# Two graph-attention layers on one core: the last block's norm moved behind the first turns of x1, sums of quarters moved off the masks, the last pair in another order

## The chip, the cores and the metric

The kernel runs on one core of a Trainium2 chip. The metric is the device time of one execution in microseconds (us), as the median of several runs. The profile shows one such execution: its span is measured from the first to the last recorded event, and the execution's own time is a little longer.

## The reference, cut to what matters

x is 4096 x 512 and adj is a 4096 x 4096 matrix of zeros and ones. Layer 0 takes, for each row, the mean over its first 64 neighbours, applies one linear map to that mean and another to the row itself, and normalises the sum. Layer 1 is an attention over all neighbours, with a residual and a norm.

```python
# layer 0
keep = Ab & (cumsum(Ab, axis=1) <= 64)
cnt = keep.sum(axis=1)
xj = leaky_relu((keep @ X) / max(cnt, 1) @ W_nb.T + b_nb)
xi = leaky_relu(X @ W_line.T + b_line)
x1 = layernorm(x + xi + where(cnt > 0, xj, 0))
# layer 1
Wh = x1 @ W + bW
e = leaky_relu((Wh @ a1 + b1)[:, None] + (Wh @ a2 + b2)[None, :], 0.2)
out = layernorm(x1 + softmax(where(adj > 0, e, -9e15), axis=1) @ Wh)
```

## The kernel before

The 4096 rows are 32 blocks of 128; two blocks make a pair (block b holds the even or the odd rows of pair b // 2). The order of work is written out by hand: each engine runs its instructions in the order of the program, and a DMA queue issues in order too. Tiles come from pools with a fixed number of buffers; a new tile waits until the last user of its buffer, or of the memory that it overlaps, is done. The stages are these.

**Layer 0.** First, y = x W_nb.T is computed block by block (L340) and kept in SBUF as a high and a low part, y_hi and y_lo. Meanwhile the adjacency is read, its running count is scanned on DVE (L179), and the kept edges are packed to bytes in DRAM (code_d). Then, for each of 32 blocks, PE multiplies the 0/1 matrix with y_hi and y_lo (L502, 64 products in four groups of 8 x 2). While block i is on PE, `finish(i - 1, g)` is run for g = 0 to 3 on DVE: mean, bias and bend (L462, L465), the sum with the block's own row, which SP loaded from own_d (L469, L497), statistics (`ln_stats`, L115, whose power -0.5 runs on POOL, L123), the scaling (L128) and the store to x1_d by POOL (L476), and two dot products with the folded attention vectors (L481), which go to the tile e12. The last block's finish is written after the loop (L509 to L510), when PE has no more products of layer 0.

**Layer 1, the slices.** The pools of layer 1 use the memory of layer 0 again. `front` holds the weights `ws` and four slots `x1s` of slices of x1. SP loads the weights (L534), the bias row bias_w (L538), and the slices (`load_turned`, four DMAs each, L553). DVE first adds the counts and writes e12's last parts (L755 to L762); POOL writes e2 and the row statistics to DRAM and reads them back as e2_n and st_n (L763 to L771), because the masks need e2 along the free dimension. Then, for 32 slices s (L780 to L805):

- PE multiplies slice s, turned, with the weights: four products of 512 columns (L786; the profile shows two records for each);
- `finish_wh(s - 1)` adds the bias on DVE (L575). For every second group of four slices it also forms the four sums of quarters of Wh (L580 to L583) that the Strassen-like products need;
- `turn_x1(s + 2)` turns a slice on DVE (L566) into one of two buffers;
- in slices 8 to 15, `mask` and `score` work on the first two blocks' weights: ACT expands the byte mask (L604), DVE subtracts it from e2_n and reduces to the maximum (L607), ACT bends the score (L596). In slices 12 to 19 `weigh` takes exponentials on ACT (L649), four slices behind; `greatest` and `shift` (L613 to L642) join the maxima of a block before its first weighing;
- in slices 22 and 26 `turn` (L668) and `combine` (L681 to L684) prepare the first two parts of the pair 0.

**Layer 1, the parts.** Each of 16 pairs has four parts q (L808 to L838). `consume(q)` runs seven products of four steps on PE (L707), which add up in four PSUM banks: products 1 and 2 share a bank, 4 and 7, 5 and 6, and 3 has its own. Next to it, DVE and ACT mask, score, weigh and turn later blocks. A pair's result is summed (`end_low`, `end_top`), divided by the sum of weights, added to the residual row (loaded by `load_res`), normalised and written (`end_row`).

**The end.** The last pair's sums and its two rows are written after the loop (L839 to L843). Its seven products stand in an order of their own:

```python
order = (1, 2, 4, 7, 5, 6, 3) if q < NP * NT - 1 else (1, 2, 6, 7, 5, 4, 3)
```

Of the kernel before, what the change touches and what calls it, by code (L numbers as in the profile page):

```python
# [20 lines left out]
P = 128  # L21
# [11 lines left out]
def two_layer_adj_gnn(  # L33
# [41 lines left out]

    two = const.tile([P, 1], F32, name="two")
    nc.vector.memset(two, 2.0)
    steep = const.tile([P, 2], F32, name="steep")
    nc.vector.memset(steep[:, 0:1], -0.5 * STEEP)
    nc.vector.memset(steep[:, 1:2], -1.5 * STEEP)  # L80
    far = const.tile([P, 1], F32, name="far")
    nc.vector.memset(far, FAR)
    neg_half = const.tile([P, 1], F32, name="neg_half")
    nc.vector.memset(neg_half, -0.5)

# [24 lines left out]

    code_d = [dram.tile([P, N // 2], BF16, name=f"code_d{b}") for b in range(NB)]

    def ln_stats(y):  # L115
        st = stat.tile([P, nc.vector.BN_STATS_DIM], F32, name="st")
        nc.vector.bn_stats(st, y)  # L117
        mv = stat.tile([P, nc.vector.BN_AGGR_DIM], F32, name="mv")
        nc.vector.bn_aggr(mv, st)
        ve = stat.tile([P, 1], F32, name="ve")  # L120
        nc.vector.tensor_scalar_add(ve, mv[:, 1:2], EPS)  # L121
        rs = stat.tile([P, 1], F32, name="rs")
        nc.gpsimd.tensor_tensor(rs, ve, neg_half, ALU.pow)  # L123
        return mv, rs
# [9 lines left out]
    with ExitStack() as l0:  # L134
# [5 lines left out]
        make_identity(nc, ident)  # L140

        late = big.tile([P, 3, C], F32, name="late")
        wa_row, bias_nb = late[:, 0:2, :], late[:, 2, :]

# [110 lines left out]
        with ExitStack() as la:  # L255
# [9 lines left out]
            def load_turned_x(i):  # L265

                if i < NB:
                    xrs[i] = late[:, i % 3, :].rearrange("p (j c) -> p j c", c=P)
                    for n in range(NC):
                        nc.gpsimd.dma_start(  # L270
                            xrs[i][ts(n, SQ)],
                            x_blk(i)[:, ts(n, P)].rearrange("(j a) c -> a j c", a=SQ),
                        )
# [36 lines left out]
            for k in range(2):  # L310
                t = early("left")
                raw["w"] += [t[:, c, :] for c in range(NC // 2)]
            rows = []
            for k in range(2):
                t = early("edge")
                rows += [t[:, c, :] for c in range(NC // 2)]

# [28 lines left out]
            def load_rows(queue):  # L346
                for k, src in enumerate((a1, a2, b_w)):
                    queue.dma_start(rows[k], src.partition_broadcast(P))
                queue.dma_start(b12[:, 0:1], b1.partition_broadcast(P))
                queue.dma_start(b12[:, 1:2], b2.partition_broadcast(P))  # L350

            def fold_w():
                for c in range(NC + 1):
                    wn = raw["w"][c] if c < NC else rows[2]
                    for k in range(2):
                        nc.vector.scalar_tensor_tensor(
                            rows[3], wn, 1.0, rows[k], ALU.mult, ALU.mult,
                            accum_out=wa[:, k, c : c + 1] if c < NC else ca[:, k : k + 1],
                        )
                nc.vector.tensor_tensor(ca, ca, b12, ALU.add)  # L360
                nc.sync.dma_start(wa_d.rearrange("k (c p) -> p k c", p=P), wa)

            def load_late():
                nc.gpsimd.dma_start(bias_nb, b_nb.partition_broadcast(P))
                nc.gpsimd.dma_start(
                    wa_row.rearrange("p k c -> p (k c)"),
                    wa_d.rearrange("k c -> (k c)").partition_broadcast(P),
                )

# [81 lines left out]
        def load_kt(b):  # L451
            if b < NB:
                assert done[0] > NCH * (b + 1) and not late_q
                ktbs[b] = ktb_p.tile([P, NT, P], BF16, name="ktb")
                nc.sync.dma_start_transpose(ktbs[b], code_d[b])

        def finish(i, g):
            if i < 0:
                return
            if g == 0:  # L460
                t = work.tile([P, C], F32, name="t")
                nc.vector.scalar_tensor_tensor(  # L462
                    t, accs.pop(i), rcnt[:, i : i + 1], bias_nb, ALU.mult, ALU.add
                )
                nc.vector.scalar_tensor_tensor(t, t, 0.01, t, ALU.mult, ALU.max)  # L465
                fin[i] = t
            elif g == 1:
                t, y = fin[i], owns.pop(i)
                nc.vector.scalar_tensor_tensor(  # L469
                    y, t, some[:, i : i + 1], y, ALU.mult, ALU.add  # L470
                )
                fin[i] = y, ln_stats(y)
            elif g == 2:
                y, stats = fin[i]
                ln_apply(y, stats)
                nc.gpsimd.dma_start(x1_blk(i), y)  # L476
            else:
                y, _ = fin.pop(i)
                for k in range(2):
                    junk = work.tile([P, C], F32, name="junk", bufs=1)  # L480
                    nc.vector.scalar_tensor_tensor(  # L481
                        junk, y, 1.0, wa_row[:, k, :], ALU.mult, ALU.mult,
                        accum_out=e12[:, 1 - k, i : i + 1],
                    )
# [3 lines left out]
        for s in range(NB * NS):  # L488
# [6 lines left out]
            if g == 2:  # L495
                owns[i] = work.tile([P, C], F32, name="own")
                nc.sync.dma_start(owns[i], own_d[i])  # L497
            kt = kts.pop(s)
# [9 lines left out]
            codes_step(start + int((s + 1) * RATE / NS))  # L508
        for g in range(NS):  # L509
            finish(NB - 1, g)  # L510

# [16 lines left out]
    NP = 4  # L528
    front = wp.tile([P, NI, NS * SQ], F32, name="w")
    ws = front[:, 0:2, :].rearrange("p a (b c) -> p (a b) c", c=C)  # L530
    x1s = front[:, 2:4, :].rearrange("p a (b c) -> p (a b) c", c=C)

    for n in range(NC):
        nc.sync.dma_start(  # L534
            ws[ts(n, SQ), :, :], w[ts(n, P), :].rearrange("(m b) c -> b m c", b=SQ)
        )
    bias_w = ep.tile([P, C], F32, name="res")
    nc.sync.dma_start(bias_w, b_w.partition_broadcast(P))  # L538
# [24 lines left out]
    def turn_x1(s):  # L563
        if s < NS:
            x1ts[s] = ep.tile([P, C], F32, name="c").rearrange("p (m i) -> p m i", i=P)
            nc.vector.transpose(  # L566
                x1ts[s].rearrange("p m (j a) -> p j m a", a=SQ),
                x1s[:, s % 4, :].rearrange("p (j m b) -> p j m b", m=NC, b=SQ),
            )

    def finish_wh(s):
# [6 lines left out]
        )  # L578
        if h == 1:
            nc.vector.tensor_tensor(b[:, 4], b[:, 1], b[:, 0], ALU.subtract)  # L580
            nc.vector.tensor_tensor(b[:, 5], b[:, 3], b[:, 4], ALU.subtract)
            nc.vector.tensor_tensor(b[:, 6], b[:, 5], b[:, 2], ALU.subtract)
            nc.vector.tensor_tensor(b[:, 1], b[:, 3], b[:, 1], ALU.subtract)  # L583
# [14 lines left out]
    def mask(b, i):  # L598

        if i == 0:  # L600
            wts[b] = wp.tile([P, NI, NS * SQ], F32, name="w")
            m4s[b] = stat.tile([P, NI], F32, name="m4", bufs=2)
# [90 lines left out]
    def consume(q):  # L693
# [7 lines left out]

        order = (1, 2, 4, 7, 5, 6, 3) if q < NP * NT - 1 else (1, 2, 6, 7, 5, 4, 3)
        for n in order:
# [9 lines left out]
    def load_res(g):  # L713

        for b in (2 * g, 2 * g + 1):
            x1rows[b] = ep.tile([P, C], F32, name="res")
            nc.sync.dma_start(x1rows[b], x1_blk(b))
# [9 lines left out]
    def end_low(g):  # L727

        p = banks[g]
        top = ep.tile([P, 2, HC], F32, name="c")  # L730
        low = ep.tile([P, 2, HC], F32, name="c")
        nc.scalar.copy(top[:, 0], p[1])
# [20 lines left out]


    cnt, idle = cnts[:, 0, :], cnts[:, 1, :]  # L755
    nc.vector.tensor_tensor(cnt, cnt, idle, ALU.add)
# [15 lines left out]


    for s in range(4):
        load_turned(s)
    load_nat(0, 0)
    load_nat(0, 1)
    turn_x1(0)
    turn_x1(1)
    for s in range(NS):  # L780
        if s > 0:
            load_turned(s + 3)
        pws[s] = ps_acc.tile([P, C], F32, name="acc")
# [5 lines left out]
        if s > 0:  # L789
            finish_wh(s - 1)  # L790
        turn_x1(s + 2)
        if FIRST <= s < FIRST + 8:
# [9 lines left out]
        if s in (FIRST + 14, FIRST + 18):  # L802
            q = (s - FIRST - 14) // 4
            turn(q)
            combine(q)  # L805
    finish_wh(NS - 1)

    for q in range(NP * NT):  # L808
# [17 lines left out]
        if b < NB:  # L826
            shift(b)
            for i in range(NI):
                weigh(b, i)
        if k == 0 and g > 0:  # L830
            end_weights(g - 1)
            end_low(g - 1)
            end_top(g - 1)
        if k == 1:
            if g > 0:
                end_row(2 * g - 2, nc.gpsimd)
                end_row(2 * g - 1, nc.gpsimd)
            load_res(g)  # L838
    end_weights(NT - 1)  # L839
    end_low(NT - 1)  # L840
    end_row(NB - 1, nc.scalar)
    end_top(NT - 1)
    end_row(NB - 2, nc.sync)  # L843

# [33 lines left out]
```

## Time and profile before

| what | value |
|---|---|
| median of 3 runs | 1620.12 us (1619.28 to 1620.49) |
| the profiled execution's own time | 1619.29 us |
| its span | 1617.5 us |
| PE busy | 1584.3 us (98%) |
| DVE busy | 1328.7 us (82%) |
| ACT busy | 902.5 us (56%) |
| POOL busy | 257.7 us (16%) |
| mean granted PE clock | 0.996 |

A busy share is an average over stages. Where the PE is busy without a gap, only fewer or shorter products would save time; where it has gaps, the wait that ended last tells what held it. A row of a timeline shows the start, the time from the start of the first to the end of the last instruction that was merged into it, engine, line, operation, tiles and shapes, and in brackets the engine's idle time before it with what released it. "SPq" rows are issues of DMAs by SP: their time is that of issuing, not of the transfer.

### The profile page before, as it was taken

The numbers are of one execution on the slowest core, as the hardware profiler recorded it, in microseconds if no ns is written. First come the engines' busy times: TensorE is split into PE (matmuls) and PEld (weight loads), VectorE is DVE, ScalarE is ACT, GpSimd is POOL, SyncE is SP. The second block draws the span as 40 slices with busy tenths as digits, with TensorE's granted clock in tenths as the row PEclk, the third lists the DMA queues.
The fourth block names the chain that finished last, engine by engine and source line by source line (L and its number), as shares of the span: only waits on it lengthen the run. The fifth ranks groups of instructions, "written<-read, shape, count | busy, mean of one in ns | idle before, by whom it ended". The sixth has DMA issues, their size and how long they took to land.

```text
span 1617.5 us, 18487 instructions
## 1 busy us (share of the span) xinstructions
PE 1584.3 (98%) x6456; PEld 1220.1 (75%) x6456; DVE 1328.7 (82%) x2183; ACT 902.5 (56%) x1054; POOL 257.7 (16%) x395
## 2 busy tenths in 40 slices
PE   9999999999999999989899999999999999999997
PEld 5444448888888787854358888888888888888886
DVE  4999987999999999847787778788888788788763
ACT  2655556677676766413337555567555567555520
POOL 4455532222222221120000000000000000000000
PEclk9999999999999999999999999999999999999999
DMA  8887878767776876352311111111111111111100
GB/s 194 282 260 240 260 210 241 217 196 210 220 212 194 217 205 187 92 130 79 92 46 27 53 40 53 40 27 53 53 40 53 40 28 52 53 40 53 40 7 33
DMA packets 168205, 192.74 MB, mean 119 GB/s; under 512 B 101376, under 2 KB 134176, under 8 KB 159920
## 3 DMA queue, kind: packets, MB, share of 16 engines
q1 hardware_dynamic: 147968, 131.51, 30.1%
q0 software_dynamic: 19712, 59.27, 10.7%
q8 instruction: 50, 0.82, 0.2%
q10 hardware_dynamic: 432, 0.79, 0.1%
q14 instruction: 43, 0.35, 0.1%
HBM read 132.65 MB, written 42.08 MB: 108 GB/s over the span
## 4 chain that ended last, share of the span: by engine, by line
PE 70%; DVE 20%; DMA 4%; issue 3%; ACT 2%; POOL 1%; SPq 0%; POOLq 0%; DVEq 0%; ACTq 0%
PE acc L707 34%; PE pt L707 14%; PE acc L340 9%; PE acc L502 9%; DVE left L179 8%; PE acc L786 4%; DVE left L184 2%; DVE junk L481 2%; DMA a<-in_adj_dram 1%; DVE st L117 1%; DVE own L469 1%; DMA late<-in_x_dram 1%; DVE t L465 1%; DVE t L462 1%; POOL rs L123 1%
## 5 line engine op out<-in xcount | busy, mean ns | idle before, releaser
L502 PE MATMUL acc<-y_hi,kt 128*128 128x512 f32 x1016 | 396.0, 390 | 3.1 <-ACT kt L249 3.1
L502 PE MATMUL acc<-y_lo,kt 128*128 128x512 f32 x1016 | 395.3, 389 | 0.0
L707 PE MATMUL acc<-bt,s 128*128 128x256 f32 x1536 | 342.3, 379 | 0.0
L707 PEld LDWEIGHTS acc<-bt,s 128*128 128x128 f32 x1536 | 291.8, 190 | 39.7
L604 ACT ACTIVATE w<-nat,far 128x1024 f32<-128x1024 uint8 x128 | 136.9, 1135 | 291.6 <-DVE a L668 238.9
L123 POOL TENSOR_TENSOR rs<-ve,neg_half 128x1 f32<-128x1 f32 x64 | 76.0, 1187 | 1026.5 <-DVE ve L121 1026.5
L707 PE MATMUL acc<-bt,a 128*128 128x256 f32 x1024 | 231.6, 379 | 0.0
L707 PE MATMUL pt<-bt,a 128*128 128x256 f32 x1024 | 231.5, 379 | 0.0
L502 PEld LDWEIGHTS acc<-y_hi,kt 128*128 128x128 f32 x1016 | 190.7, 188 | 44.9 <-ACT kt L249 5.3
L502 PEld LDWEIGHTS acc<-y_lo,kt 128*128 128x128 f32 x1016 | 190.7, 188 | 39.4
L707 PEld LDWEIGHTS pt<-bt,a 128*128 128x128 f32 x1024 | 194.6, 190 | 26.9 <-issue 0.5
L707 PEld LDWEIGHTS acc<-bt,a 128*128 128x128 f32 x1024 | 194.6, 190 | 26.5
L668 DVE STREAM_TRANSPOSE a<-w 128x1024 f32<-128x1024 f32 x128 | 153.0, 1225 | 59.4 <-ACT w L649 52.7
L167 ACT ACTIVATE edge<-a,steep 128x2048 bf16<-128x2048 int32 x64 | 127.9, 1998 | 104.5 <-DVE left L184 82.4
L249 ACT ACTIVATE kt<-ktb,steep 128x1024 fp32r<-128x1024 uint8 x124 | 139.4, 1147 | 82.0 <-PE acc L502 64.9
L596 ACT ACTIVATE w<-w,st_n 128x1024 f32<-128x1024 f32 x128 | 149.4, 1233 | 50.7 <-DVE m L607 50.7
L607 DVE CUSTOM_DVE_ANT_0 w<-e_n,w 128x1024 f32<-128x1024 f32 x128 | 149.5, 1221 | 4.3 <-ACT w L604 2.9
L649 ACT ACTIVATE w<-w,nm 128x1024 f32<-128x1024 f32 x128 | 145.4, 1137 | 11.3 <-DVE nm L640 11.3
L179 DVE TENSOR_TENSOR_SCAN left<-two,edge 128x2048 bf16<-128x2048 f32 x32 | 141.3, 4417 | 12.0 <-ACT edge L167 10.9
L179 DVE TENSOR_TENSOR_SCAN left<-two,ends,edge 128x2048 bf16<-128x2048 f32 x32 | 143.2, 4476 | 0.0
L786 PE MATMUL acc<-w,c 128*128 128x512 f32 x256 | 113.6, 602 | 14.9 <-DVE c L566 14.9
L202 ACT CAST code<-left 128x2048 uint8<-128x2048 bf16 x64 | 120.6, 1884 | 7.6 <-DVE left L184 7.6
(114 smaller groups left out, 1529.3 us busy)
## 6 DMA issues: line engine op xcount, KB each, us to landing
a<-in_adj_dram SPq DMA_DIRECT2D x64, 1024.0 KB, 6.0
code_d<-code POOLq DMA_DIRECT2D x64, 256.0 KB, 5.3
nat<-code_d SPq DMA_DIRECT2D x256, 64.0 KB, 2.0
own_d<-xb POOLq DMA_DIRECT2D x32, 256.0 KB, 6.0
own<-own_d SPq DMA_DIRECT2D x32, 256.0 KB, 2.7
x_d<-own POOLq DMA_DIRECT2D x32, 256.0 KB, 2.6
w<-x_d SPq DMA_DIRECT2D x128, 64.0 KB, 2.0
res<-x_d SPq DMA_DIRECT2D x32, 256.0 KB, 2.8
```

Source lines behind the costliest of these rows:

```text
L167: nc.scalar.activation(edge_of[s], loaded.pop(s), AF.Sigmoid, bias=steep[:, 0:1], scale=STEEP, accum_out=cnts[:, h, b : b + 1],)
L179: nc.vector.tensor_tensor_scan(left, two.to_broadcast([P, CH]), e, NEIGHBORS + 2.0 if h == 0 else end, ALU.max, ALU.subtract,)
L249: nc.scalar.activation(kts[s], bytes_.rearrange("p t (i r) -> p t r i", r=2), AF.Sigmoid, bias=steep[:, 1:2], scale=STEEP,)
L340: nc.tensor.matmul(pl, lhs_t[:, k, :], w_t[name][:, k, :], start=(k == 0), stop=(k == NC - 1),)
L502: nc.tensor.matmul(accs[i], kt[:, k // 2, k % 2, :], term[:, j, :], start=(j == 0 and term is y_hi), stop=(j == NB - 1 and term is y_lo),)
L596: nc.scalar.activation(dst, src, AF.Prelu, bias=bias, scale=scale, alpha=0.2)
L604: nc.scalar.activation(w_i, nats[b, i // 2].bitcast(U8)[:, i % 2, :], AF.Relu, bias=far, scale=-FAR)
L607: nc.vector.tensor_tensor_reduce(w_i, e2_n, w_i, 1.0, -3e38, ALU.subtract, ALU.max, m4s[b][:, i : i + 1])
L649: nc.scalar.activation(w_i, w_i, AF.Exp, bias=nms[b][:, i : i + 1], accum_out=z4s[g][:, r, i : i + 1])
L668: nc.vector.transpose(a[:, r].rearrange("p s (i a) -> p i s a", a=SQ), wts[2 * g + r][:, :, ts(k, 8 * SQ)].rearrange("p i (s x) -> p i s x ...
L707: nc.tensor.matmul(banks[g][n], lhs[:, j, :], bt[:, 4 * k + j, rhs, :], start=(k == 0 and j == 0 and n == mate[0]), stop=(k == NP - 1 and ...
L786: nc.tensor.matmul(pws[s], x1t[:, m, :], ws[:, m, :], start=(m == 0), stop=(m == NC - 1))
```

## The change

Five things change. First, the norm of the last block: after the loop of layer 0 nothing is finished any more. Instead, after the definitions of layer 1, SP loads the first four slices, then block 31's own row, then the first masks; DVE turns slices 0, 1 and 2; and only then `finish(31, g)` follows, with temporary rows in a tile `early` of layer 1, whose first halves take the three turned slices. Second, turned slices have three buffers (a pool `rows`, which in layer 0 holds the three rows that were the tile `late`), and a slice is turned three ahead; its load is issued seven ahead. Third, `finish_wh` only notes the quarter; the four sums are formed by `combine_wh`, once in each slice from 16 on other than 22 and 26, and what is left after block 2's weighing in part 0. Fourth, in the last part product 4 comes first, `end_weights` before the end, and the last pair's sums and norms are written out: the upper row is worked on in halves, between the steps of the lower row, and is written by two DMAs. Fifth, small moves: constants in one tile, wa_row in two loads, residual rows of even blocks in `rows`.

```diff
+    rows = ctx.enter_context(tc.tile_pool(name="rows", bufs=3, reuse_waits="tile"))
+    late = [rows.tile([P, C], F32, name="c") for _ in range(3)]
+    wa_rows, bias_nb = late[0:2], late[2]
...
             def load_late():
                 nc.gpsimd.dma_start(bias_nb, b_nb.partition_broadcast(P))
-                nc.gpsimd.dma_start(
-                    wa_row.rearrange("p k c -> p (k c)"),
-                    wa_d.rearrange("k c -> (k c)").partition_broadcast(P),
-                )
+                for k in range(2):
+                    nc.gpsimd.dma_start(wa_rows[k], wa_d[k].partition_broadcast(P))
...
             if g == 2:
-                owns[i] = work.tile([P, C], F32, name="own")
-                nc.sync.dma_start(owns[i], own_d[i])
+                if i < NB - 1:
+                    owns[i] = place("own")
+                    nc.sync.dma_start(owns[i], own_d[i])
...
-        for g in range(NS):
-            finish(NB - 1, g)
...
     front = wp.tile([P, NI, NS * SQ], F32, name="w")
+    early = wp.tile([P, NI, NS * SQ], F32, name="w")
+    spare += [early[:, i, C:] for i in (0, 2, 3)]
+    owns[NB - 1] = early[:, 1, C:]
...
     def turn_x1(s):
         if s < NS:
-            x1ts[s] = ep.tile([P, C], F32, name="c").rearrange("p (m i) -> p m i", i=P)
+            t = early[:, s, :C] if s < 3 else rows.tile([P, C], F32, name="c")
+            x1ts[s] = t.rearrange("p (m i) -> p m i", i=P)
...
         if h == 1:
+            later.append(kk)
+
+    later = []
+
+    def combine_wh():
+
+        if later:
+            b = bt[:, later.pop(0)]
             nc.vector.tensor_tensor(b[:, 4], b[:, 1], b[:, 0], ALU.subtract)
             nc.vector.tensor_tensor(b[:, 5], b[:, 3], b[:, 4], ALU.subtract)
             nc.vector.tensor_tensor(b[:, 6], b[:, 5], b[:, 2], ALU.subtract)
...
-        order = (1, 2, 4, 7, 5, 6, 3) if q < NP * NT - 1 else (1, 2, 6, 7, 5, 4, 3)
+        order = (1, 2, 4, 7, 5, 6, 3) if q < NP * NT - 1 else (4, 1, 2, 6, 7, 5, 3)
...
+    for s in range(4):
+        load_turned(s)
+    nc.sync.dma_start(owns[NB - 1], own_d[NB - 1])
+    load_nat(0, 0)
+    load_nat(0, 1)
+    for s in range(3):
+        turn_x1(s)
+        load_turned(s + 4)
+    for g in range(4):
+        finish(NB - 1, g)
...
-    turn_x1(0)
-    turn_x1(1)
     for s in range(NS):
-        if s > 0:
-            load_turned(s + 3)
...
-        turn_x1(s + 2)
+        turn_x1(s + 3)
+        load_turned(s + 7)
...
+        elif s >= FIRST + 8:
+            combine_wh()
     finish_wh(NS - 1)
...
+        while q == 0 and later:
+            combine_wh()
...
+        if q == NP * NT - 1:
+            end_weights(g)
...
-    end_weights(NT - 1)
-    end_low(NT - 1)
-    end_row(NB - 1, nc.scalar)
-    end_top(NT - 1)
-    end_row(NB - 2, nc.sync)
+    p, rz = banks[NT - 1], rzs[NT - 1]
+    top, low = (rows.tile([P, 2, HC], F32, name="c") for _ in range(2))
+    x_top, x_low = x1rows[NB - 2].rearrange("p (h c) -> p h c", h=2), x1rows[NB - 1]
+    stt = nc.vector.scalar_tensor_tensor
+    st = stat.tile([P, 2, nc.vector.BN_STATS_DIM], F32, name="st2", bufs=1)
+    nc.scalar.copy(top[:, 0], p[1])
+    tt(top[:, 1], top[:, 0], p[6], ALU.add)
+    tt(top[:, 0], top[:, 0], p[2], ALU.add)
+    tt(low[:, 0], top[:, 1], p[7], ALU.add)
+    stt(top[:, 0], top[:, 0], rz[:, 0:1], x_top[:, 0], ALU.mult, ALU.add)
+    nc.vector.bn_stats(st[:, 0], top[:, 0])
+    tt(low[:, 1], low[:, 0], p[5], ALU.add)
+    tt(low[:, 0], low[:, 0], p[4], ALU.subtract)
+    y_low = low.rearrange("p h c -> p (h c)")
+    stt(y_low, y_low, rz[:, 1:2], x_low, ALU.mult, ALU.add)
+    low_stats = ln_stats(y_low)
+    tt(top[:, 1], top[:, 1], p[5], ALU.add)
+    stt(top[:, 1], top[:, 1], rz[:, 0:1], x_top[:, 1], ALU.mult, ALU.add)
+    stt(top[:, 1], p[3], rz[:, 0:1], top[:, 1], ALU.mult, ALU.add)
+    nc.vector.bn_stats(st[:, 1], top[:, 1])
+    mv, rs = ln_rs(st)
+    ln_apply(y_low, low_stats)
+    nc.scalar.dma_start(out_blk(NB - 1), y_low)
+    for h in range(2):
+        ln_apply(top[:, h], (mv, rs))
+        (nc.sync, nc.scalar)[h].dma_start(out_blk(NB - 2)[:, ts(h, HC)], top[:, h])
```

## The prediction

> **What bounds the kernel now.** I read the page first: PE is busy for 1584.3 of 1617.5 us, so only its gaps can be saved. Its row for the products of layer 1's first stage names a gap and who ended it:
>
> ```profile
> L786 PE MATMUL acc<-w,c 128*128 128x512 f32 x256 | 113.6, 602 | 14.9 <-DVE c L566 14.9
> ```
>
> The timeline of PE from 700 to 842 us puts these 14.9 us in place. The bracket is the idle time before the row and what ended it; 8 records are one slice of x1.
>
> ```profile
> 713.38 53.33 PE L786 MATMUL acc<-w,c 128*128 128x512 f32 x120 [7.72 <-DVE c L566]
> 768.28 3.70 PE L786 MATMUL acc<-w,c 128*128 128x512 f32 x8 [1.58 <-DVE c L566]
> ...
> 786.72 20.87 PE L786 MATMUL acc<-w,c 128*128 128x512 f32 x48 [0.65 <-DVE c L566]
> 809.36 14.00 PE L786 MATMUL acc<-w,c 128*128 128x512 f32 x32 [1.77 <-DVE c L566]
> 823.55 10.57 PE L786 MATMUL acc<-w,c 128*128 128x512 f32 x24 [0.19 <-DVE c L566]
> ```
>
> The same stretch of DVE, and of SP, shows what came before the first turn:
>
> ```profile
> 705.70 0.75 DVE L462 SCALAR_TENSOR_TENSOR t<-acc,rcnt,late 128x512 f32<-128x512 f32 x1 [8.34 <-PE acc L502]
> ...
> 712.62 1.29 DVE L566 STREAM_TRANSPOSE c<-w 128x512 f32<-128x512 f32 x2
> 718.67 0.71 DVE L566 STREAM_TRANSPOSE c<-w 128x512 f32<-128x512 f32 x1 [4.76 <-PE acc L786]
> ```
>
> ```profile
> 705.46 0.35 SPq L538 DMA_DIRECT2D res<-in_L_gnn_bW_dram  x1
> 705.86 7.74 SPq L553 DMA_DIRECT2D w<-x_d  x16
> 713.64 6.12 SPq L591 DMA_DIRECT2D nat<-code_d  x8
> ```
>
> SP's rows are the catch. The load of bias_w (L538) takes space that y_hi held, so it waits for layer 0's last products (705.4), and all turned loads of x1 stand behind it. The changed program's order of instructions has that wait still, on the same product. Last, DVE at the end:
>
> ```profile
> 1604.30 0.42 DVE L733 TENSOR_TENSOR c<-c,acc 128x256 f32<-128x256 f32 x1 [17.76 <-PE acc L707]
> ...
> 1605.97 0.42 DVE L735 TENSOR_TENSOR c<-c,acc 128x256 f32<-128x256 f32 x1 [0.80 <-PE acc L707]
> ...
> 1613.70 0.55 DVE L128 TENSOR_SCALAR c<-c,mv,rs 128x512 f32<-128x512 f32 x1 [0.73 <-POOL rs L123]
> ```
>
> From 834 us to 1607.7 PE has no gap: 64 parts of 12.08 us. Nothing there is to be saved.
>
> **Part 1, the transition.** Removed from ahead of the first turn: the norm of block 31 and the counts, 705.70 to 712.6. In its place the first turn waits for its four loads. Of the 16 issues (7.74 us, 0.48 each) slice 0's last goes at 707.3 and lands some 2.9 us later: 710.2. With a turn of 0.65, PE starts at 710.9 instead of 713.38. Slice 1 lands at about 711.4, slice 2 at 713.4; the third turn ends at 714.05. Only then can DVE begin the norm (705.70 before). Block 31's own row is now issued behind the 16 (713.64) and lands 2.7 later, 716.3, where L469's successor would want it at 715.55: 0.75 lost. The norm's 6.1 us and the counts' 0.8 then end at 721.7, turn 3 at 722.4.
>
> PE: slice 0 took 5.2 us before (713.38 until the turn at 718.67, which waits for its end), the later ones 3.435. [...] The new gap is 5.2 us[...]. Cold: slices 0 to 2 end at 716.1, 719.5, 723.0, and slice 3 starts at 723.0. Warm: they end by 721.2 and slice 3 waits for turn 3 until 722.4. [...] Slice 4 needs turn 4, whose load is issued behind the eight loads of nat. Before, it landed at 725.7, which gives turn 4 at 726.7 with 0.35 of SP's added issue; if those loads land faster, since e2's small writes move from 713 to 722, PE decides, 725.9 to 726.4. I take slice 4 at 726.6. Before it was 728.97. **Gain 2.4 us, bounds 1.8 to 3.1**, not 7.7.
>
> The norm is 8.35 us later, and behind it on DVE and POOL stand e2's writes and loads. Before: L762 ended at 712.7, the first load of e2_n issued at 720.78, the last landed at about 726.6, 13.9 later. Now 721.7 + 13.9 = 735.6. The first mask reads e2_n at 746.77 - 2.4 = 744.4. It is covered by 8.8 us. The x1 store stays ahead of e2 on POOL; x1's last quarter is read only from slice 24.
>
> **Part 2, the masks (slices 8 to 31).** On the old clock, E(s) being the end of slice s: E(8) = 746.14, and 23 slices of 3.435 would end at 825.15; the next stage starts at 833.96. So 8.8 us are lost. Two things work against them. A third buffer lets turn s+3 run when slice s has ended, so a turn may be late by 6.2 us instead of 2.7. And the four sums of a quarter (L580 to L583, 1.59 us from start to start) leave slices 13 to 16, to run from 16 on.
>
> What does not go: with weighing, the mask steps are a circle DVE reduce, ACT score, ACT weigh, ACT mask, each waiting for the last: 768.85 to 773.56 is 4.71 us, with DVE idle 0.67 before each L607. Without the sums DVE merely idles longer. The reduces stay at 761.06, 768.85, 773.56, 778.27. Turns 16 to 19 then end at 766.6, 771.25, 775.95, 780.65 (L575 0.6, turn 0.65), against slices due at 770.2, 773.6, 777.0, 780.5: PE waits 0.2, where it lost about 6.3 up to 786.72. Then comes the greatest of block 1 (1.7), ACT's lm (1.3) and one sum: DVE is at 785.4. Turn 20 ends at 786.65, its slice was due at 784.1: 2.6 lost.
>
> From here DVE has no idle time: 0.6 + 0.65 + 1.6 = 2.85 per slice against PE's 3.435, and 6.35 in slices 22 and 26, which turn and combine a part (L668 2.33, L681 to L684 2.75). Slice 17 begins on DVE at 785.4; 17 to 21 are 5 x 2.85, 799.65; 22 to 806.0; 23 to 25 to 814.55; 26 to 820.9; 27 to 823.75. Turn 25 is at 800.9 (due 803.8), turn 30 at 822.15 (due 821.05): 1.1 lost. E(31) = 829.05. PE's losses are 0.2 + 2.6 + 1.1 = 3.9 of 8.8. **Gain 4.9 us, bounds 2.5 to 6.5**: the lower if DVE's steps each run 5% longer over its 54 us of unbroken work, the upper if the greatest's wait overlaps.
>
> Given back? Two of the 16 sums are still left after slice 31 and go behind block 2's weighing. DVE leaves slice 31 at 833.8, ends four reduces at 838.5, greatest and shift at 841.7, the sums at 844.9, turn and combine of part 2 at 850.1. PE needs them at 829.05 + 24.17 = 853.2: covered by 3.1 us. Part 3: 861.7 against 865.3. Part 4: 870.6 against 877.4. If that cover failed, the excess would be paid once.
>
> **Part 3, the last pair.** Product 5 moves from fifth to sixth. Products 5 and 6 share a bank, and L733 waited for 5 (1604.2), so the first sum starts at 1605.97, 1.7 later. Against it, the last chain is reordered. Start to start, dependent halves take 0.45, others 0.34, full rows 0.75: twelve steps bring the lower row's statistics to 1610.7, the upper row's halves and statistics to 1612.7, pow on POOL to 1613.6 (0.3 + 0.58), the lower row's scaling fills that wait, and two halves of 0.33 follow. The last output DMA is issued at about 1614.3; it was 1614.28. It carries 128 KB instead of 256, which landed in 2.0[...]. **Gain 0.1, bounds -0.5 to 0.8.**
>
> **At nothing:** the constants in one tile; the three rows moved to a pool of their own, whose users in layer 0 have the same waits as before; one more POOL issue of 0.55 in load_late near 230 us, when PE is busy throughout; the new buffers for residual rows, three allocations for each pair in a ring of three, so each comes free where it did. Beside such jitter, layer 0 is the same: bounds -0.5 to 0.5.
>
> **Sum.** 2.4 + 4.9 + 0.1 = 7.4. The profiled execution took 1619.29 with a span of 1617.5; the span becomes 1610.1, its time 1611.9. The median of the runs is 0.8 above the profiled one: 1612.7.
>
> **The rivals.**
> A: DVE's backlog spends the third buffer. For: DVE is saturated from slice 16. Against: its needs are 2.85 a slice against 3.435. If the mask circle or PSUM reads lengthen by 10% over 54 us, 4 to 5 us of part 2 are gone: 1617.0, chance 0.11.
> B: No stall at slices 20 and 30, because DVE gets through earlier than I add up, and slice 0 warm: 1608.5, chance 0.12.
> C, slower: e2 comes late. The norm now waits for loads of x1, and behind it POOL's chain for e2_n meets the turned loads; DVE, which waits for e2_n in order, holds up every turn and sum behind it. Against: 8.8 us of cover, and then the gain has to be spent. It decides from a landing of about 752, that is 30 us after the counts instead of 13.9; 4 us beyond that give 1624. Chance 0.03.
> D: The change doesn't do what it says: the turns stay behind the blocked SP queue (as I read it) and the loads, with later traffic, land 2 us later too, so that only half of part 2 is left: 1616.0, chance 0.06.
> The main case has 0.68.
>
> **Range and chances.** Main case 1610.5 to 1615. Leaving out C, the tip of A and of B gives 1609.3 to 1616.5. A difference of 0.2% is 3.2 us, about what a measurement can tell from none; the bound lies at 1616.9. Faster: main, B, most of D and part of A, 0.88. Same: 0.09. Slower: 0.03.
>
> **What would show it.** PE's first L786 step (now L809) near 710.9 with some 5.2 us idle before it, right; near 706, SP was not blocked; the norm's L462 step starting near 714 behind three turns; slice 4 near 726.6; idle of PE at two places in the slices from 19 on, about 4 us in sum; the first product of the part stage near 826.7; no gap of PE in parts 2 to 4; the first sum of the tail 1.7 later after the last part's start, and the last issue about 6.6 after the last product, as before. Gaps of PE in slices 13 to 18 would say that the circle matters to PE after all; a wait for e2_n at the first mask speaks for C.

## The result and the profile after

The changed kernel takes 1612.45 us (median of 6 runs, 1611.63 to 1613.51) against 1620.3 us before (6 runs): a ratio of 0.995, 95% interval 0.9937 to 0.9963. Its profiled execution took 1611.63 us with a span of 1609.9 us, 7.6 less than before.

The timeline of PE over the same stretch as before (bracket: idle time ahead of the row, and what ended it; 8 records are one slice):

```profile
709.69 13.46 PE L809 MATMUL acc<-w 128*128 128x512 f32 x24 [5.47 <-DVE w L575]
722.98 55.10 PE L809 MATMUL acc<-w,c 128*128 128x512 f32 x128
778.41 3.70 PE L809 MATMUL acc<-w,c 128*128 128x512 f32 x8 [0.34 <-DVE c L575]
784.35 41.87 PE L809 MATMUL acc<-w,c 128*128 128x512 f32 x96 [2.24 <-DVE c L575]
826.06 3.62 PE L724 MATMUL pt<-bt,a 128*128 128x256 f32 x16
```

Of the seven waits that such rows showed after slice 0 before the change, two are left, at slices 19 and 20, and the gap ahead of slice 0 is 2.2 us shorter. But the first row has 24 records, three slices, in 13.3 us, where 10.3 would do.

To compare the parts I need a common point near the end of layer 0. That is the issue of the bias row's load, which waits for layer 0's last product. SP after:

```profile
704.02 0.35 SPq L546 DMA_DIRECT2D res<-in_L_gnn_bW_dram  x1
704.41 7.56 SPq L561 DMA_DIRECT2D w<-x_d  x16
712.06 0.38 SPq L777 DMA_DIRECT2D w<-own_d  x1
```

It still stands ahead of x1's loads, as before: SP issued in the order of the program, at 704.02, 704.41 and 712.06. A second common point is the end of slice 8, which releases a turn on DVE; the two rows are from before and from after:

```profile
746.14 0.71 DVE L566 STREAM_TRANSPOSE c<-w 128x512 f32<-128x512 f32 x1 [0.56 <-PE acc L786]
```

```profile
743.78 0.71 DVE L575 STREAM_TRANSPOSE c<-w 128x512 f32<-128x512 f32 x1 [2.15 <-PE acc L809]
```

Between these points the two executions differ so (us):

| stretch | before | after | difference | forecast |
|---|---|---|---|---|
| start to bias row's issue (layer 0) | 705.46 | 704.02 | -1.44 | 0 |
| to the end of slice 8 (746.14, 743.78) | 40.68 | 39.76 | -0.92 | -2.4 |
| to the first product of the parts (833.96, 826.06) | 87.82 | 82.28 | -5.54 | -4.9 |
| to the end of the span | 783.54 | 783.84 | +0.30 | -0.1 |
| sum | 1617.5 | 1609.9 | -7.6 | -7.4 |

The second row is less than the shorter gap promised. The granted clock of PE tells why (columns: stretch, its length, PE busy and records, PEclk, DMA share, GB/s). Before:

```profile
705.66:709.72 4.06, 0.00 (x0) 1.00 0.52 158
709.72:713.38 3.66, 0.00 (x1) 0.50 0.68 188
713.38:716.55 3.17, 3.17 (x4) 0.50 0.97 133
```

After:

```profile
704.21:708.71 4.50, 0.00 (x1) 1.00 0.53 159
708.71:709.69 0.98, 0.00 (x1) 0.50 0.48 136
709.69:715.53 5.84, 5.84 (x7) 0.50 0.51 152
```

In both, the clock halves some 4 us after PE fell idle (4.06 and 4.50) and stays so for 6.8 us. Before, PE was idle for 3.66 of these; after, for 0.98. The earlier start was spent at half clock.

DVE after, behind the first turns, and then at the end (with ACT's queue, which issues the last output):

```profile
712.34 0.71 DVE L468 SCALAR_TENSOR_TENSOR w<-acc,rcnt,c 128x512 f32<-128x512 f32 x1
...
715.73 0.75 DVE L475 SCALAR_TENSOR_TENSOR w<-w,e 128x512 f32<-128x512 f32 x1 [1.96 <-DMA w<-own_d]
...
721.01 0.70 DVE L575 STREAM_TRANSPOSE c<-w 128x512 f32<-128x512 f32 x1
```

```profile
1598.14 0.42 DVE L877 TENSOR_TENSOR c<-c,acc 128x256 f32<-128x256 f32 x1 [19.49 <-PE acc L724]
...
1606.12 0.73 DVE L131 TENSOR_SCALAR c<-c,mv,rs 128x256 f32<-128x256 f32 x2 [0.44 <-POOL rs L126]
...
1606.89 0.35 ACTq L896 DMA_DIRECT2D out_dram<-c  x1
```

The norm starts behind three turns and waits 1.96 for its own row; turn 3 follows the counts. In the tail the last part starts at 1587.52, as long after the first product of the parts as before (761.46 and 761.45). The first sum starts 10.62 later, and the last output is issued 8.75 after that; the one wait that DVE's rows show on the way is 0.44, for POOL.

### The profile page after: what moved, and what is told of

Its sections match the earlier page's. It is cut to its first block, busy times and chain, and to the rows that moved or that the text cites. A ratio compares the mean times of both kernels' runs of the same rounds, so it can differ in the third digit from the quotient of the medians.

```text
span 1609.9 us, 18503 instructions
## 1 busy us (share of the span) xinstructions
PE 1583.8 (98%) x6456; PEld 1221.9 (76%) x6456; DVE 1328.1 (82%) x2186; ACT 903.2 (56%) x1054; POOL 258.1 (16%) x396
## 4 chain that ended last, share of the span: by engine, by line
PE 69%; DVE 23%; DMA 3%; issue 2%; ACT 1%; POOL 1%; SPq 0%; DVEq 0%; POOLq 0%; ACTq 0%
PE acc L724 34%; PE pt L724 14%; DVE left L179 10%; PE acc L340 9%; PE acc L509 9%; PE acc L809 3%; DVE left L184 2%; DVE junk L487 2%; DVE own L475 1%; DVE st L117 1%; DVE t L471 1%; DMA a<-in_adj_dram 1%; DVE t L468 1%; DVE own L131 1%; DVE c L575 1%
## 5 line engine op out<-in xcount | busy, mean ns | idle before, releaser
L724 PEld LDWEIGHTS acc<-bt,s 128*128 128x128 f32 x1536 | 292.3, 190 | 39.2
L621 ACT ACTIVATE w<-nat,few 128x1024 f32<-128x1024 uint8 x128 | 136.9, 1135 | 277.1 <-DVE a L685 237.0
L126 POOL TENSOR_TENSOR rs<-ve,few 128x1 f32<-128x1 f32 x64 | 76.1, 1190 | 1021.1 <-DVE ve L124 1021.1
L249 ACT ACTIVATE kt<-ktb,few 128x1024 fp32r<-128x1024 uint8 x124 | 139.8, 1148 | 84.7 <-PE acc L509 69.0
L167 ACT ACTIVATE edge<-a,few 128x2048 bf16<-128x2048 int32 x64 | 127.9, 1998 | 99.4 <-DVE left L184 78.0
L179 DVE TENSOR_TENSOR_SCAN left<-few,edge 128x2048 bf16<-128x2048 f32 x32 | 141.3, 4416 | 12.3 <-ACT edge L167 11.2
L179 DVE TENSOR_TENSOR_SCAN left<-few,ends,edge 128x2048 bf16<-128x2048 f32 x32 | 143.2, 4476 | 0.0
L340 PE MATMUL acc<-wt_nb,xt 128*128 128x512 f32 x256 | 115.4, 594 | 1.8 <-DVE xt L294 1.0
```

What stands on the lines that cost most here:

```text
L167: nc.scalar.activation(edge_of[s], loaded.pop(s), AF.Sigmoid, bias=steep[:, 0:1], scale=STEEP, accum_out=cnts[:, h, b : b + 1],)
L179: nc.vector.tensor_tensor_scan(left, two.to_broadcast([P, CH]), e, NEIGHBORS + 2.0 if h == 0 else end, ALU.max, ALU.subtract,)
L249: nc.scalar.activation(kts[s], bytes_.rearrange("p t (i r) -> p t r i", r=2), AF.Sigmoid, bias=steep[:, 1:2], scale=STEEP,)
L340: nc.tensor.matmul(pl, lhs_t[:, k, :], w_t[name][:, k, :], start=(k == 0), stop=(k == NC - 1),)
L621: nc.scalar.activation(w_i, nats[b, i // 2].bitcast(U8)[:, i % 2, :], AF.Relu, bias=far, scale=-FAR)
L724: nc.tensor.matmul(banks[g][n], lhs[:, j, :], bt[:, 4 * k + j, rhs, :], start=(k == 0 and j == 0 and n == mate[0]), stop=(k == NP - 1 and ...
```

## Experiments

My theory after the result: the masks' gain comes from the third buffer, the transition's from loads that still wait for the bias row, and what the earlier start should have brought went into the half clock. The rivals were that the sums put off are what pays, that the norm on DVE still holds the slices, and that layer 0's edits count. Below, "first part" is the first product of the parts, less the bias row's issue: 122.04 after, 128.50 before. Each group of runs has a chip and runs of before of its own: 1621.84 (first four experiments), 1621.67 (next four), 1620.83 (next three); the last has 1621.38. Across the groups it is the ratio to before that can be compared; the changed kernel's is 0.995.

### The sums formed at once again

```diff
         if h == 1:
             later.append(kk)
+            combine_wh()
...
-        elif s >= FIRST + 8:
-            combine_wh()
```

> The changed kernel with the four sums of a quarter formed at once again, in finish_wh; the third buffer for turned slices stays. Theory (the third buffer carries the masks' gain, the deferral next to nothing, because DVE waits 2.2 us for ACT before each masked maximum anyway): 1612.5 us, within 1 us of the changed kernel, PE idle in the slices about 2 to 3 us in sum as before the undoing, first part product 82 to 83 us after the end of slice 8. Rival (the deferral carries it): the stalls of slices 15 to 19 come back, 5 to 6 us, so about 1617.5 us.

1613.47 us, 0.9946 (0.9933 to 0.9958). First part 121.07. PE:

```profile
778.26 3.70 PE L810 MATMUL acc<-w,c 128*128 128x512 f32 x8 [0.65 <-DVE c L575]
782.97 3.70 PE L810 MATMUL acc<-w,c 128*128 128x512 f32 x8 [1.01 <-DVE c L575]
787.31 41.47 PE L810 MATMUL acc<-w,c 128*128 128x512 f32 x96 [0.64 <-DVE c L575]
```

The waits fall elsewhere but sum to 2.30, against 2.58. Putting the sums off brings nothing that shows once there are three buffers.

### The norm back at the end of layer 0

```diff
             codes_step(start + int((s + 1) * RATE / NS))
+        for g in range(NS):
+            finish(NB - 1, g)
...
-    for g in range(4):
-        finish(NB - 1, g)
```

> The changed kernel with the last block's norm put back ahead of the turns (its own row loaded in layer 0's loop as before). Theory (the turns wait for SP's blocked loads, so the norm's move is worth little): first slice product 1 to 1.5 us later after layer 0's last product than in the changed kernel (7 instead of 5.7), and in all 0 to 1.5 us slower, 1612.5 to 1614, where the length of PE's slow clock at the start decides. Rival (moving the norm is worth the 7.7 us gap): 1617 to 1620.

1614.51 us, 0.9951 (0.9937 to 0.9964). The gap is 6.88 instead of 5.47, but the half clock then takes only 3.2 us of the slices instead of 5.8, and the first part stands at 122.15: 0.1 later than in the first profile of the changed kernel, 0.8 later than in the one below. The norm's move is worth under 1 us.

### The old tail

The order (1, 2, 6, 7, 5, 4, 3) and the old calls for the last two rows.

> The changed kernel with the last pair as it was: products 1, 2, 6, 7, 5, 4, 3 and the sums and norms in the old order. Theory (the new tail lost 0.3 us in the profile, 783.84 against 783.54 from the first part product to the end): 1612.2, 0.3 us faster or the same; first tail sum 1.7 earlier. Rival (the new tail gains what it was written for, a shorter last chain): 1 to 2 us slower, 1613.5 to 1614.5.

1613.16 us, 0.9941 (0.9929 to 0.9953). From the first product of the parts to the end it needs 783.51, the new tail 783.84. So the new tail shows a cost of 0.3 us in the profiles, which the times can't tell from nothing.

### x1's loads ahead of the bias row

This run frees two things together: the loads of bias_w and of the first masks are written behind those of x1, and the buffer of the first turns is put where the adjacency lay instead of y_hi (the memset only fixes which buffer that is):

```diff
     early = wp.tile([P, NI, NS * SQ], F32, name="w")
+    other = wp.tile([P, NI, NS * SQ], F32, name="w")
-    nc.sync.dma_start(bias_w, b_w.partition_broadcast(P))
+    nc.gpsimd.memset(other[:, 0, 0:1], 0.0)
...
-    load_nat(0, 0)
-    load_nat(0, 1)
     for s in range(3):
         turn_x1(s)
         load_turned(s + 4)
+    nc.sync.dma_start(bias_w, b_w.partition_broadcast(P))
+    load_nat(0, 0)
+    load_nat(0, 1)
```

> The changed kernel, with the load of bias_w and of the first masks behind the loads of x1, and the tile for the first turned slices on memory that layer 0's adjacency tiles held, not y_hi (one cell of another tile is set by POOL to fix which buffer it gets). Theory (the wait of the bias row for y_hi holds the transition): the three turns end before layer 0's last product, PE's gap falls from 5.5 us to under 0.5, its clock stays full (3 us more), slice 8 ends some 31.5 us after layer 0 instead of 39.8: 1604 to 1605. Rival (the masks wait for e2 or DVE in any case, so an earlier start is lost again in slices 8 to 20): 1610 to 1612.5.

1606.01 us, 0.9898 (0.9884 to 0.9911). SP and PE:

```profile
683.68 9.91 SPq L562 DMA_DIRECT2D w<-x_d  x16
...
705.61 0.35 SPq L782 DMA_DIRECT2D res<-in_L_gnn_bW_dram  x1
```

```profile
705.64 10.46 PE L811 MATMUL acc<-w 128*128 128x512 f32 x24
...
777.32 43.16 PE L811 MATMUL acc<-w,c 128*128 128x512 f32 x96 [2.23 <-DVE c L576]
```

The 16 loads of slices 0 to 3 are issued 22 us ahead of the bias row, and slice 0 starts at 705.64 with no gap and at full clock; the first part is 7.3 earlier, at 114.71. How much of that either of the two edits would bring alone, no run shows. The last row takes 43.16 for the same 96 records that took 41.87 after the change. The clock behind the wait of 2.23 shows it:

```profile
777.32:777.70 0.38, 0.38 (x1) 1.00 0.00 0
777.70:781.12 3.42, 3.42 (x5) 0.51 0.30 84
```

Here a wait of 2.23 us brought 3.42 us at half clock. A wait of the same length (2.24) brought none in the changed kernel (PEclk 1.00 behind it). So the length of a wait alone doesn't set its price; what else does, no run shows.

### The changed kernel again

> The changed kernel as it is, for comparison on one chip with the kernels of this group. Both theories: about 1612.5 us, ratio to before 0.995; slices 0 to 2 take about 13.3 us from the first slice product to slice 3, with a slow-clock stretch of 5 to 6 us; masks lose 0.3 and 2.2 us on PE at slices 19 and 20. If the slow clock's length depends on where the gap falls rather than on its length, those 13.3 us differ by a microsecond or so from the first profile.

1613.35 us, 0.995 (0.9936 to 0.9963). The bias row is issued at 706.06, 2.0 later than in the first profile of the same kernel: layer 0 alone scatters by that. Slices 0 to 2 take 12.66 instead of 13.29, since 4.51 us of half clock fall on them and not 5.84.

### The sums put off, without the third buffer

The kernel before, with `later` and `combine_wh` alone.

> The kernel before with one part of the change: the sums of quarters of wh are put off the masks, with two buffers for turned x1 as before and all else as before. Theory (the masks' pace is set by the circle VectorE, score, weigh, mask on ScalarE, and the buffers, not the sums, cost PE the time): the putting-off alone gives nothing, 1620 us, within 1 us of before, and PE still loses 6 to 9 us at slices 16 to 20. Rival (the sums on VectorE are what delays the turns): most of the 5.5 us gained there after the change shows up, 1615 to 1616 us.

1621.13 us, 0.9996 (0.9988 to 1.0004): the theory's number. PE still waits at six places:

```profile
772.26 3.70 PE L793 MATMUL acc<-w,c 128*128 128x512 f32 x8 [0.96 <-DVE c L566]
...
781.68 3.70 PE L793 MATMUL acc<-w,c 128*128 128x512 f32 x8 [1.01 <-DVE c L566]
787.61 20.87 PE L793 MATMUL acc<-w,c 128*128 128x512 f32 x48 [2.23 <-DVE c L566]
```

With another 1.01 between these rows and 0.19 and 0.59 further on, the waits sum to 5.99, of 7.18 before. With the first experiment (buffer without putting off: 2.30) this leaves the third buffer as what pays, together with the earlier loads and turns that go with it, which no run separates from it.

### PE kept busy in the gap

Six more products ahead of slice 0, whose result nothing uses:

```diff
+    warm = ps_s.tile([P, C], F32, name="pt")
+    for m in range(6):
+        nc.tensor.matmul(
+            warm, ws[:, m % 4, 0:P], ws[:, m % 4, :], start=(m == 0), stop=(m == 5)
+        )
     for s in range(NS):
```

> The changed kernel with six more matrix products (two quarters of wh's weights with themselves, result unused) put on PE between the last product of layer 0 and slice 0, some 5.2 us at full clock, so that PE is busy in the gap. Theory (the slow clock after the gap is the reason why slices 0 to 2 take 13.3 us): they take 10.4 us at full clock up to the turn that slice 3 needs (done about 17.7 us after the last product of layer 0), so slice 3 starts about 1.3 us earlier relative to the end of layer 0 and the time falls by about 1.3 us, to 1611. Rival (slices 0 to 2 are held by the turns behind the norm and not by the clock): slice 3 starts at the same place, no gain; 1612.5.

1613.62 us, 0.9949 (0.9937 to 0.9962): the rival's number.

```profile
706.06 5.31 PE L807 MATMUL pt<-w 128*128 128x512 f32 x12
711.63 10.57 PE L814 MATMUL acc<-w 128*128 128x512 f32 x24 [0.26 <-DVE w L575]
724.84 55.20 PE L814 MATMUL acc<-w,c 128*128 128x512 f32 x128 [2.64 <-DVE c L575]
```

The clock stays full and three slices take 10.57, so the slow clock was real. But slice 3 then waits 2.64 for turn 3, which ends 18.7 us after the bias row's issue; slice 3 started 18.2 to 19.0 after it with the half clock. In the two profiles of the changed kernel turn 3 was done 17.7 and 18.1 after it. (Here the third turn got its load 1.7 later than in the second of them, and turn 3 came 0.6 later. In the profiles without the added products the 16 issues took from 7.56 us (the changed kernel, first) to 8.93 (the old tail), so this need not be the products' doing.) So two limits lie about a microsecond apart or less (1.3 and 0.1), and taking one away shows the other.

### The mask's first step one slice ahead

ACT's L621 of the next mask is written ahead of the score of the mask at hand:

```diff
-            mask(b, i)
+            if s == FIRST:
+                far_of(b, i)
+            near_of(b, i)
+            if s < FIRST + 7:
+                far_of(*divmod(s + 1 - FIRST, NI))
             score(b, i)
```

(`far_of` is the ACT half of `mask`, `near_of` the DVE half.)

> The changed kernel with ScalarE's first step of each mask (L621) written one slice ahead, before the score of the mask at hand, so that VectorE's scan no longer waits for score, weigh and mask in a row. Theory (that circle of 4.71 us sets the pace of masks 5 to 8): the pace falls to ScalarE's own 3.7 us, VectorE's waits of 2.2 us fall to under 1.2, PE's stalls at slices 19 and 20 (0.34 and 2.24) go, first part product about 2.5 us earlier, 1610. Rival (VectorE's own load sets it): the stalls stay within 0.5 us of 2.6 and the time at 1612.5.

1610.45 us, 0.993 (0.9918 to 0.9943); its five runs end at 1610.88, where those of the changed kernel beside it begin at 1612.74. First part 118.17, 3.2 ahead of the changed kernel beside it (121.37). DVE's reduces in the changed kernel, and then here:

```profile
766.48 1.22 DVE L624 CUSTOM_DVE_ANT_0 w<-e_n,w 128x1024 f32<-128x1024 f32 x1 [2.21 <-ACT w L621]
...
771.19 1.22 DVE L624 CUSTOM_DVE_ANT_0 w<-e_n,w 128x1024 f32<-128x1024 f32 x1 [2.26 <-ACT w L621]
```

```profile
766.37 1.18 DVE L631 CUSTOM_DVE_ANT_0 w<-e_n,w 128x1024 f32<-128x1024 f32 x1
...
768.71 1.18 DVE L631 CUSTOM_DVE_ANT_0 w<-e_n,w 128x1024 f32<-128x1024 f32 x1
...
771.96 1.23 DVE L631 CUSTOM_DVE_ANT_0 w<-e_n,w 128x1024 f32<-128x1024 f32 x1 [0.67 <-ACT w L625]
```

```profile
725.74 99.73 PE L816 MATMUL acc<-w,c 128*128 128x512 f32 x232
825.30 3.62 PE L731 MATMUL pt<-bt,a 128*128 128x256 f32 x16
```

Steps of 4.71 become 2.3 and 3.25, and the 29 slices from slice 3 on run as one row without a wait. So the circle had set the pace, and the pace was all that was left of the masks' loss.

### The last pair's sums sooner

Products in the order (1, 2, 5, 6, 4, 7, 3), and the sums that need only 1, 2, 5 and 6 first.

> The changed kernel with the last pair's products in the order 1, 2, 5, 6, 4, 7, 3 and the sums that need only products 1, 2, 5 and 6 written first. Theory (the new tail gains nothing because its first sum waits for both products of bank 2, the sixth product of seven, and VectorE's 8.7 us of sums and norms then run alone behind PE): the first sum starts two products (3 us) sooner, the last output is issued about 2.3 us sooner, 1611. Rival (the end hangs on product 3 and the norm behind it, whatever the order): last issue within 0.5 us of before it, 1613.

1610.25 us, 0.9932 (0.9918 to 0.9945).

```profile
1596.14 0.42 DVE L877 TENSOR_TENSOR c<-c,acc 128x256 f32<-128x256 f32 x1 [16.03 <-PE acc L724]
...
1599.54 0.42 DVE L883 TENSOR_TENSOR c<-c,acc 128x256 f32<-128x256 f32 x1 [0.95 <-PE acc L724]
```

The last part starts at 1588.98: the first sum comes 7.16 after it instead of 10.62, the last issue (1605.49) 16.51 instead of 19.37. That is 2.9 us, where the theory had 2.3. (No runs of the changed kernel stand in this group.)

### The three together

> The changed kernel with three edits of this study together: x1's turned loads and turns not held by the bias row (no gap at slice 0), ScalarE's first mask step one slice ahead (no stalls at slices 19 and 20), and the sooner sums of the last pair. Theory (the three act at different places and add: 7.3 us, 2.9 us and the 1.3 us that the slow clock took behind the stall at slice 20, 2.3 us): about 1600 us. Rival (with slices 0 to 2 sooner another limit comes up, e2_n's landing or the transfers of codes): 1603 to 1606 us.

1598.02 us, 0.9859 (0.9845 to 0.9872), better than either kernel.

```profile
706.20 10.46 PE L818 MATMUL acc<-w 128*128 128x512 f32 x24
716.50 99.73 PE L818 MATMUL acc<-w,c 128*128 128x512 f32 x232
816.07 3.62 PE L732 MATMUL pt<-bt,a 128*128 128x256 f32 x16
```

From layer 0 through all 32 slices PE has no wait. The first part stands at 109.90, 12.1 earlier than after the change, and the rest of the span is 2.9 shorter. The three add: 12.1 is the 7.3 of the freed loads and the 4.8 that the waits and the half clock still cost the slices in that run.

### Early loads, but the norm first

> As the run without the bias row ahead of x1's turned loads (1606 us), but with the norm of block 31 back at the end of layer 0, ahead of the first turns on VectorE. Theory (moving the norm gains nothing as long as the loads come after the bias row, but is what lets the turns be done ahead once the loads come early): the turns wait behind the norm, a gap of 6 to 8 us at slice 0 comes back with its slow clock, 1613 to 1614 us. Rival (the norm's place is worth nothing in either case, the loads alone count): no gap, 1606 us.

1613.75 us, 0.9956 (0.9943 to 0.997). The loads are being issued at 689.88, 22 us ahead of slice 0, and yet:

```profile
711.89 12.39 PE L805 MATMUL acc<-w 128*128 128x512 f32 x24 [6.88 <-DVE w L575]
```

This gap is that of the norm at layer 0's end with late loads, to the hundredth. The norm holds the turns whether x1 is there or not. Moving the norm alone and freeing the loads alone are worth under 1 us and nothing, and both together over 7 us.

### Layer 0's rows as before

> The changed kernel with the norm of block 31 back at the end of layer 0 (as in the earlier run of that, 0.995 of before) and, besides, layer 0's rows where they were before: one tile of three rows in layer 0's own pool, one load for both rows of wa. The medians of the runs differ by about 8 us, the parts that the two profiles show from the end of layer 0 on only by 6 to 6.5. Theory (that rest is the scatter of layer 0, which reaches 3.5 us between the profiled executions, and not these edits): about 1614.5 us and a ratio to before within 0.001 of 0.995. Rival (the moved rows and the split load make layer 0 1.5 us faster): 1616 us, 0.996.

1613.05 us, 0.995 (0.9937 to 0.9964): layer 0's edits do nothing that shows. So the difference between the medians (8.3 us in the second group) and the parts of the profiles behind layer 0 (6 to 6.5) isn't theirs. The profiled execution of before (1619.29) and that of the sums put off alone (1618.99, where the runs went to 1622.84) stand at the low end of their kernels' runs; in the second group the 17 runs of before scatter from 1619.55 to 1624.68, while the changed kernel's five stay within 1.6 us. So some 2 us of the difference between the medians have no cause that a profile here shows; this stays open.

## Why the prediction was right, and where it was not

**The sum** (7.4 forecast, 7.6 measured) was right in part by luck. 1.44 of the 7.6 are layer 0, which the forecast had within 0.5, and the transition brought 0.92, below its bounds of 1.8 to 3.1; the two errors nearly cancel. In thirteen profiled executions of this study layer 0 ends (the bias row is issued) between 704.0 and 707.6 us, so a single pair of profiles can't hold layer 0 within 0.5. Without it the parts give 6.2 of 7.4.

**Part 1, the transition: the mechanism right, one term mis-sized.** The step "all turned loads of x1 stand behind it" held: a gap of 5.47 where 5.2 was forecast, not the disappearance of 7.7. The run with the loads and the turns' buffer freed shows the 7.3 us that these waits withhold. The term that failed is the price of the slow clock, which was my estimate. I took over the 1.8 us that slice 0 lost behind the old gap (5.2 against 3.435) and had them fall on slice 0 alone (the forecast's "cold"; "warm" is slice 0 without that loss), and so came to a price of 0.6 us (slice 3 at 723.0 against 722.4). Slices 0 to 2 lost 3.0 (13.29 against 10.30), so that slice 3 started 18.96 us after the bias row's issue, where 723.0 - 705.46 = 17.5 was forecast. Measured from stretches of a quarter of a microsecond, the half clock behind the gaps is this (us):

| kernel | gap | clock halves after idle for | slow for | of it on slices |
|---|---|---|---|---|
| before | 7.72 | 4.06 | 6.83 | 3.17 |
| sums put off alone | 7.72 | 4.58 | 6.83 | 3.69 |
| norm back at layer 0's end | 6.88 | 3.26 | 6.83 | 3.22 |
| changed | 5.47 | 4.50 | 6.83 | 5.84 |
| changed, again | 5.32 | 3.00 | 6.83 | 4.51 |

Behind each of these gaps the slow time is the same, counted from its onset. A shorter gap moves PE's restart into it, and half of each microsecond won is lost again: 5.84 us cost 2.9, where 3.17 cost 1.6. That is why 2.25 us of gap became 0.92.

The run with PE kept busy adds that the clock was not alone: turn 3 was done only 1.3 and 0.1 us before slice 3 could start. That turn was mis-sized too. The norm started 8.3 after the bias row's issue (8.6 forecast), but block 31's row took 3.6 us to land, not 2.7, so the norm waited 1.96 for it and not 0.75, and turn 3 was done at 17.7 instead of 722.4 - 705.46 = 16.9. The cover of e2_n held: the first mask starts 40.4 after the bias row's issue, without a wait for it.

**Part 2, the masks: right.** Losses against 23 slices of 3.435 fell from 8.8 to 3.3, where 3.9 were forecast. The places were the forecast's: from start to start of the slices PE lost 0.5 at slice 19 (forecast 0.2), 2.5 at slice 20 (2.6) and 0.4 at slice 30 (1.1). The last is too short for the timeline's bracket, but turn 30 ended at 819.03 and the next product started at 819.09, 0.73 after the one before instead of 0.43:

```profile
818.33 0.70 DVE L575 STREAM_TRANSPOSE c<-w 128x512 f32<-128x512 f32 x1
```

DVE had begun slice 17's work 39.2 after the end of slice 8, just as forecast (785.4 - 746.14), but then went at 2.78 a slice (785.77 to 788.55) instead of 2.85, which saves 0.8 by turn 30. "Without the sums DVE merely idles longer" held to the letter: 2.2 us idle before each reduce instead of 0.67, with the reduces 4.71 apart; and the run with the sums formed at once loses no more. The circle itself was shown by taking L621 out of it.

**Part 3, the tail: the sign was wrong by little.** The first sum came 1.73 later after the last part's start (10.62; before, 1604.30 - 1595.41 = 8.89), as forecast. The chain behind it was mis-sized by 0.4: from the first sum to the last issue it took 8.75 instead of 1614.3 - 1605.97 = 8.3. Nearly all of that had arisen by the end of the upper row's statistics, which came 7.1 after the first sum instead of 6.7. So the last issue came 0.5 later instead of about the same, and 0.2 came back in the smaller last transfer, which landed in 1.8 us instead of 2.0. +0.3 lies inside the bounds.

**The rivals.** A (DVE's backlog) did not come; B did not come (slice 20 stalled as forecast, slice 30 for 0.4 instead of 1.1, and slice 0 was slow); C did not come; D's premise that SP stays blocked was right, as in the main case, but nothing of the masks' gain was lost.

## What to carry to other kernels

When PE's gap is shortened but not closed, count the clock: compare the granted clock in stretches before and after, since here 2.25 us off the gap brought only 0.92 us. A blocked queue and a norm ahead of the same turn were two limits on one start: removing either alone showed under 1 us, removing both over 7. And where an engine has slack, giving it less to do moved nothing that shows (the sums put off alone: 0.9996 of before); look for the circle of waits that it stands in, and take one step out of that circle.

## What the runs showed of the hardware

I had not expected that the half clock behind gaps of 5.2 to 7.7 us would last 6.83 us in each of the ten profiles read for it, from an onset 3.0 to 4.6 us after PE fell idle, with PE busy for up to 5.8 of them; nor that a wait of 2.23 us would bring 3.42 us of half clock in one execution and one of 2.24 none in another.
